# Two-layer block kernel: three quantised blocks of each batch made in earlier loops and passed through DRAM, and the weights' quantiser moved to another tile ring

## The chip, the cores and the metric

The kernel runs on one NeuronCore of a Trainium2 chip. The metric is the device time of one execution in microseconds (us). The engines are named as the profile names them: PE (TensorE, matrix products), DVE (VectorE), ACT (ScalarE), POOL (GpSimd) and SP (SyncE, which here only issues DMAs).

## The reference

The input x has 2 batches of 4096 tokens with 512 channels, in float32. Two layers follow each other; each adds two branches, which read the same layer norm, to the residual stream. Of the first layer the second branch is what the change is about:

```python
xn = _layernorm(x, axis=-1)
x = x + _L0_attn_ref(xn, ...) + _L0_ffn_ref(xn, L0_ffn_weight, L0_ffn_bias)
xn = _layernorm(x, axis=-1)
x = x + _L1_attn_ref(xn, ...) + _L1_ffn_ref(xn, ...)
# _L0_attn_ref: (ssm(silu(conv3(xn @ w1.T + b))) * silu(xn @ v1.T + b)) @ w2.T + b
# _L0_ffn_ref:  per token, blocks of 32 channels:
scales = jnp.maximum(jnp.max(jnp.abs(blocks), axis=-1) / 7.5, eps)
q = _nearest_on_grid(blocks / scales[..., None], _GRID)     # 6-bit floats
out = (xq * xs) @ (wq * ws).T + bias       # x and the weight quantised alike
# _L1_attn_ref: linear attention (16 heads, relu q and k), residual, layer norm
# _L1_ffn_ref:  sigmoid(xr @ Wr.T) * (relu(xk @ Wk.T) ** 2 @ Wv.T), xr and xk mixed with the token before
```

## The kernel before, in words

Tokens are handled in blocks of T = 512 (four tiles of 128 tokens, TJ = 4): NB = 8 blocks a batch, NK = 16 in all. The program has these stages, one after the other.

1. The first stage (the loop `for n in range(NK)`, to about 462 us) turns the normalised block (`turned`), multiplies it with w1 and v1 (`projected`, L338 and L353 take the results out of the accumulator banks on ACT), convolves the block before (`convolved`) and stores the results to DRAM. In iterations 9 to 12 it also quantises the second branch's weight, a quarter each (`quantised_weight`), and in iterations 6 to 13 the eight tiles of blocks 0 and 1 of batch 0 (`quantised`).
2. The recurrence of the state space model (to about 635 us).
3. For each batch: `mixed` computes the first layer's sum x1 block by block (`branch`, L629, is the quantised product; `x1_of` adds the product with w2, L644, and takes the bank out with L651 on POOL and L652 on DVE), normalises it and multiplies it with Wk and the keys' sums (`summed`, L675; L706 and L707 make the keys). `pairs` computes the queries and the second layer's ffn keys for two blocks at a time. `layer1` finishes the second layer, one block of 512 tokens at a time (`at_block(i)` is called at the head of each), and stores the output.

`quantised(n, j, dst, temp)` makes one tile of 128 tokens in four steps, as a generator: load the tile `xq` (L367, SP); normalise it in four pieces on ACT (L126) and find the scales of its blocks (L174 to L177 on DVE) and scale it (L178, POOL); round it (L186 to L191 on DVE, L192 on POOL); transpose it on DVE (L374) into `dst`. `quantised_weight` does the same with a tile `w_y` of the weight (L359, L362).

Where a tile is quantised: for batch 0, blocks 0 and 1 in the first stage; for batch 1, block 0 in `pairs` of batch 0 (`at_pair`). All other blocks are quantised in `mixed` itself. There a small planner sets the order: `clock` starts at -8 and `tick()` adds one, and each step of tile j of block m is due at `2 * TJ * (m - 2) + 2 * j - 2 + step`. What is due before the clock's start comes at once:

```python
clock, events = [-2 * TJ], defaultdict(list)
...
for m in range(ahead, NB):
    for j in range(TJ):
        q = quantised(b * NB + m, j, partial(xd_of, m, j), t2q)
```

`ahead` is the number of blocks that come ready made (2 for batch 0, 1 for batch 1). For these, `mixed` begins the banks with the quantised product (`branch`) before anything else.

Tiles come from rings of a fixed number of slots; a new tile waits until the slot's last user is done. Those that matter: `yv`, eight tiles of 128 x 512 (the diff calls it by that name; two are `heads`, four are `xd0`, the rest serve `xq` and the loads of `gated`); `xc`, four tiles in the first stage, used by the convolution and by `w_y`; `xe`, two tiles in the first stage, the scratch of the rounding; `t2q`, two tiles, the scratch of the rounding in the later stages and of `mixed_r` in `pairs`; `t8`, five tiles of 1 MB, for whole blocks.

A compiler orders each engine's instructions from the program's order and its own estimate of when operands are ready, so that an instruction may stand before others that the source has earlier. The trace shows it: the first tile `xq`, due in iteration 6, is loaded at 80.7 us, when the loop is in iteration 2. On each engine the order is then fixed, and an instruction that waits holds those behind it. SP issues all loads and most stores, ACT the stores of `projected` and `pairs`.

Of the kernel before, what the change touches and what calls it, by code (L numbers as in the profile page):

```python
# [10 lines left out]
F32 = mybir.dt.float32  # L11
# [32 lines left out]
def block_kernel(ctx: ExitStack, tc: tile.TileContext, a: dict, out: bass.AP):  # L44
# [28 lines left out]
    sd1 = dram.tile([NK, P, TJ, 2], F32, name="sd1")  # L73
    qd = dram.tile([NK, CC, P, T], F32, name="qd")
    kd = dram.tile([NK, CC, P, T], F32, name="kd")

    def bank(tag="mm", bufs=2):
        return ps.tile([P, D], F32, tag=tag, name=f"p_{tag}", bufs=bufs)
# [276 lines left out]
        return x1  # L355

    def quantised_weight(work, o):
        y = work.tile([P, D], F32, tag="xc", name="w_y", bufs=4)
        nc.sync.dma_start(out=y, in_=a["ffn_w"][o])  # L359
        s = mx_scaled(y)  # L360
        mx_rounded(y, s, work.tile([P, D], F32, tag="xe", name="w_c"))
        nc.vector.transpose(wd[:, :, o * P : (o + 1) * P], y)  # L362

    def quantised(n, j, dst, temp):

        xq = yv.tile([P, D], F32, tag="yv", name="xq")
        nc.sync.dma_start(out=xq, in_=a["xi"][n * TJ + j])  # L367
        yield
        laid_normalised(xq, mvi[:, :, n, j, :])
        scales = mx_scaled(xq)  # L370
        yield
        mx_rounded(xq, scales, temp())
        yield
        nc.vector.transpose(dst().rearrange("p c t -> p (c t)"), xq)  # L374
        yield

    def convolved(work, n, x1, ccs=range(CC)):
# [156 lines left out]
    def mixed(b, z0, xds, xnTs, mvs, w2, wk):  # L534
# [6 lines left out]
        def xd_of(m, j):  # L541
# [2 lines left out]
                xds[m] = [xd[:, jj] for jj in range(TJ)]  # L544
            return xds[m][j]

        clock, events = [-2 * TJ], defaultdict(list)
# [117 lines left out]
        def summed(i, j, xn, kt):  # L667
# [6 lines left out]
            for c in range(CC):  # L674
                nc.tensor.matmul(  # L675
                    pg[c], lhsT=xn[:, c * P : (c + 1) * P], rhs=kt, start=first, stop=last
                )

        x_of(0)
        x_of(1)  # L680
        for i in range(ahead):

            pos[i] = [bank(("mm", "tr")[i]) if j < 2 else acc() for j in range(TJ)]
            for j in range(TJ):
                branch(i, j, pos[i][j])
                if i == 0:
                    tick()
        x1_of(0)
        for i in range(NB):
            xn = xts[i]  # L690
            for j in range(TJ):
                rescaled(xn[j], xn[j], mvs[:, i, j, :])
            if i + 1 < NB:
                x1_of(i + 1)
            else:
                for _ in range(TJ):
                    tick()
            if i == 0:
                first_x1_turned(xn)
            xnT = xnTs[i]  # L700
            for j in range(TJ):
                tj = slice(1 + j * P, 1 + (j + 1) * P)
                pk = bank("tr")
                product(pk, lambda k: xnT[:, k, tj], lambda k: wk[:, k, :])
                kt = t2("k")
                nc.vector.tensor_tensor(kt, pk, bk, ALU.add)  # L706
                nc.scalar.activation(kt, kt, AF.Relu)  # L707
                flush()
                later.append(partial(summed, i, j, xn[j], kt))
                gate(i + 2, j)  # L710
                tick()
            if i + 2 < NB:
                x_of(i + 2)
# [112 lines left out]
    def pairs(b, xnTs, wq, wk, made, kvx, at_pair):  # L826
# [37 lines left out]
        def mixed_r(p):  # L864
            for n in range(2):
                xnT = xnTs[2 * p + n]
                for c in range(CC):
                    t = t2q()
                    nc.scalar.activation(t, xnT[:, c, 0:T], AF.Copy, scale=om_r[:, c, :])
                    nc.vector.scalar_tensor_tensor(  # L870
                        xnT[:, c, 1 : T + 1], xnT[:, c, 1 : T + 1], mu_r[:, c, :], t,
                        ALU.mult, ALU.add,
                    )
# [103 lines left out]
    with tc.tile_pool(name="tab", bufs=1) as tab:  # L977
# [3 lines left out]
        with pool("a", 2) as work, pool("pm", 1) as pm:  # L981
# [31 lines left out]
            made = []  # L1013
            powers = chunk_powers(pm, made)
            xd0 = [yv.tile([P, CC, P], F32, tag="yv", name=f"xd{j}") for j in range(TJ)]
            for n in range(NK):
                if 0 < n < NK - 1:
                    xi = laid(work, n + 1)
                if n + 3 < NK:
                    xts[n + 3] = fetched(work, n + 3)  # L1020
                before, x1 = x1, projected(work, n, xnT, x1)
                if n + 2 < NK:
                    measured(n + 2, xts.pop(n + 2))
                    spread_out(mvi[:, :, n + 2], sd[n + 2], mv0[:, n + 2])
                if n + 1 < NK:
                    xnT = turned(work, n + 1, xi)
                if 0 < n < NK - 1:
                    convolved(work, n - 1, before)
                if n in (2, 3, 8):
                    next(powers)  # L1030
                elif 4 <= n < 4 + CC:
                    chunk_tables(*made, n - 4)
                elif 9 <= n < 9 + CC:
                    quantised_weight(work, n - 9)
                if 6 <= n < 6 + 2 * TJ:

                    m, j = divmod(n - 6, TJ)
                    if m == 1 and j == 0:
                        xd_b1 = by_tile(single.tile([P, CC * (T + 1)], F32, name="wide"))
                    for _ in quantised(  # L1040
                        m, j, lambda: xd_b1[:, j] if m else xd0[j],
                        lambda: work.tile([P, D], F32, tag="xe", name="c"),
                    ):
                        pass
                if n == NK - 2:
                    b_out = load_row("w2_b")
                    ffn_b = work.tile([P, D], F32, tag="xe", name="ffn_b")
                    nc.sync.dma_start(out=ffn_b, in_=a["ffn_b"].partition_broadcast(P))
                    nc.gpsimd.tensor_tensor(b_out, b_out, ffn_b, ALU.add)
                    bk, gamma, beta = (load_row(s) for s in ("bk", "gamma", "beta"))  # L1050
                    bq, mu_r, mu_k = column("bq"), column("mu_r"), column("mu_k")
                    om_r = const.tile([P, CC, 1], F32, name="om_r")
                    om_k = const.tile([P, CC, 1], F32, name="om_k")
                    nc.vector.tensor_scalar(om_r, mu_r, -1.0, 1.0, ALU.mult, ALU.add)
                    nc.vector.tensor_scalar(om_k, mu_k, -1.0, 1.0, ALU.mult, ALU.add)
# [7 lines left out]
    z0 = t8()  # L1063
    for cc in range(CC):
        gated(0, 0, z0, cc)
    xds = {0: xd0, 1: [xd_b1[:, j] for j in range(TJ)]}

    for b in range(B):
        mvs = stay.tile([P, NB, TJ, 2], F32, tag="mvs", name="mvs")
# [5 lines left out]
        c_wts = []  # L1075
        if b + 1 < B:
            xd0 = [yv.tile([P, CC, P], F32, tag="yv", name=f"xd{j}") for j in range(TJ)]
            ahead = [quantised((b + 1) * NB, j, lambda j=j: xd0[j], t2q) for j in range(TJ)]

        def at_pair(p, half):  # L1080

            if b + 1 < B and p < TJ:
                for _ in range(2):
                    next(ahead[p])

        def at_block(i):
            if b + 1 < B and i == NB - 1:
                next_in.append(t8())
                for cc in range(CC):
                    gated(b + 1, 0, next_in[0], cc)  # L1090
# [2 lines left out]
        pairs(b, xnTs, wq, wk1, made, kvx, at_pair)  # L1093
        layer1(b, xnTs, mvs, kvx, [load_weight(s) for s in ("W_r", "W_v")], at_block)
        if b + 1 < B:
            z0, xds = next_in[0], {0: xd0}
            c_wts = [load_weight("w2_w"), load_weight("Wk")]


# [59 lines left out]
```

## Time and profile before

| | us |
|---|---|
| median of 3 runs | 2420.28 |
| lowest and highest | 2420.0, 2421.31 |
| the profiled execution | 2425.51 |
| its span, first to last instruction | 2423.7 |
| mean granted clock of PE | 0.993 |

The page of the profile has the busy time of each engine over the span; PE's matrix products and its weight loads (PEld) overlap. The stages in this execution: the first to 462 us, the recurrence to 635, `mixed` of batch 0 to 1065, `pairs` to 1262, `layer1` to 1512, and for batch 1 `mixed` to 1970, `pairs` to 2170, `layer1` to the end. A group of instructions is written as line, engine, operation, out<-in, shapes and count, then busy us, mean ns of one, and the engine's idle time just before them with what ended it. In a list of waits, "PE p_mm L629 <- DVE x L652" is read: PE's instruction of line 629, which writes the tile p_mm, could start only when DVE's of line 652 was done.

### The profile page before, as it was taken

Reading aid. Unit: us, or ns where it says so; the run is one execution under the profiler, and the core shown is the slowest. Engines: PE = TensorE matmul, PEld = TensorE weight load, DVE = VectorE, ACT = ScalarE, POOL = GpSimd, SP = SyncE. Lnnn points to the kernel's source line nnn. Section 1 sums busy time; section 2 is a strip of 40 time slices with the busy share of each in tenths; the row PEclk is TensorE's granted clock in tenths of the full one; section 3 lists DMA queues with packets and bytes.
Section 4 is the critical chain, followed back from the end, with each engine's and each line's share of the span. In section 5 each row is a group of like instructions: output and inputs, shape, how many; then the busy total and the mean of one; then the engine's idle time right before and its main releaser. Section 6 shows DMA issues by size and latency. Waiting matters only on the chain.

```text
span 2423.7 us, 21898 instructions
## 1 busy us (share of the span) xinstructions
PE 2366.3 (98%) x6400; PEld 1112.2 (46%) x6400; DVE 1545.7 (64%) x3092; ACT 1018.1 (42%) x1940; POOL 466.7 (19%) x447
## 2 busy tenths in 40 slices
PE   7999999999989999999999999799999999999999
PEld 3444443466434444444445554344444444445554
DVE  7856457565596662257658779865662265557777
ACT  5777664344342332246662223232332146662222
POOL 1000012122253331110001114333331110001111
PEclk9999999999999999999999999899999999999999
DMA  7746432477743332202264344533332202263331
GB/s 241 222 122 214 143 122 93 134 213 264 261 143 113 109 116 85 66 27 91 87 250 155 119 141 147 169 109 109 110 121 75 66 26 87 83 226 133 131 128 61
DMA packets 250521, 321.83 MB, mean 133 GB/s; under 512 B 55712, under 2 KB 117152, under 8 KB 249376
## 3 DMA queue, kind: packets, MB, share of 16 engines
q1 hardware_dynamic: 221312, 253.30, 33.0%
q10 hardware_dynamic: 29088, 67.12, 7.1%
q8 instruction: 51, 0.84, 0.1%
q14 instruction: 70, 0.57, 0.1%
HBM read 202.23 MB, written 118.12 MB: 132 GB/s over the span
## 4 chain that ended last, share of the span: by engine, by line
PE 64%; DVE 5%; issue 1%; POOL 0%; DMA 0%; ACT 0%; POOLq 0%; DVEq 0%
PE p_acc L152 16%; PE p_tr L152 9%; PE p_acc L675 8%; PE p_mm L629 7%; PE p_acc L797 7%; PE p_mm L644 7%; PE p_mm L797 6%; PE p_tr L797 2%; PE p_mm L924 1%; PE p_tr L924 1%; DVE xq L190 0%; DVE t L532 0%; DVE x L960 0%; DVE t L944 0%; POOL xq L178 0%
## 5 line engine op out<-in xcount | busy, mean ns | idle before, releaser
L152 PE MATMUL p_acc<-xnT,w_v_w 128*128 128x512 f32 x512 | 227.5, 603 | 8.1 <-ACT x L338 8.1
L675 PE MATMUL p_acc<-k,x 128*128 128x512 f32 x512 | 230.2, 593 | 3.2 <-ACT k L707 3.2
L152 PE MATMUL p_acc<-xnT,w_w_w 128*128 128x512 f32 x512 | 226.0, 600 | 5.9 <-DVE mv L122 5.0
L152 PE MATMUL p_acc<-w_W_v,t 128*128 128x512 f32 x512 | 222.3, 593 | 0.0
L629 PE MATMUL p_mm<-w_d,t 128*128 128x512 f32 x416 | 193.9, 609 | 16.3 <-DVE x L652 16.3
L152 PE MATMUL p_acc<-w_W_r,xnT 128*128 128x512 f32 x448 | 201.4, 593 | 0.0
L644 PE MATMUL p_mm<-w_w_w,t 128*128 128x512 f32 x448 | 201.1, 593 | 0.0
L152 PE MATMUL p_tr<-w_Wk,xnT 128*128 128x512 f32 x448 | 199.1, 593 | 0.0
L945 POOL TENSOR_TENSOR x<-x,row_beta 128x512 f32<-128x512 f32 x64 | 83.9, 1312 | 578.9 <-ACT xn L126 575.8
L152 PEld LDWEIGHTS p_acc<-xnT,w_v_w 128*128 128x128 f32 x512 | 98.9, 194 | 134.2 <-issue 120.3
L386 DVE SCALAR_TENSOR_TENSOR xc<-x,col_conv_w,xc 128x512 f32<-128x512 f32 x128 | 92.2, 767 | 106.4 <-POOL x L328 95.3
L152 PEld LDWEIGHTS p_acc<-xnT,w_w_w 128*128 128x128 f32 x512 | 98.5, 193 | 130.8 <-issue 119.5
L675 PEld LDWEIGHTS p_acc<-k,x 128*128 128x128 f32 x512 | 97.2, 190 | 126.5 <-issue 119.6
L673 POOL TENSOR_TENSOR ksum<-ksum,k 128x512 f32<-128x512 f32 x62 | 83.8, 1352 | 370.0 <-ACT k L707 370.0
L152 PEld LDWEIGHTS p_acc<-w_W_v,t 128*128 128x128 f32 x512 | 97.5, 190 | 122.2 <-issue 119.4
L109 ACT ACTIVATE rs_s<-rs_v 128x4 f32<-128x4 f32 x48 | 9.5, 204 | 339.6 <-DVE rs_v L107 339.4
L706 DVE TENSOR_TENSOR k<-p_tr,row_bk 128x512 f32<-128x512 f32 x64 | 43.8, 684 | 162.1 <-PE p_tr L152 162.1
L951 ACT ACTIVATE r<-p_acc 128x512 f32<-128x512 f32 x64 | 38.2, 597 | 253.3 <-PE p_acc L152 240.0
L629 PEld LDWEIGHTS p_mm<-w_d,t 128*128 128x128 f32 x416 | 80.5, 196 | 118.5 <-issue 96.6
L644 PEld LDWEIGHTS p_mm<-w_w_w,t 128*128 128x128 f32 x448 | 85.4, 191 | 107.2 <-issue 107.0
L152 PEld LDWEIGHTS p_tr<-w_Wk,xnT 128*128 128x128 f32 x448 | 85.3, 190 | 107.0 <-issue 104.3
L652 DVE TENSOR_TENSOR x<-x,p_mm 128x512 f32<-128x512 f32 x56 | 38.3, 684 | 147.9 <-PE p_mm L644 147.9
(217 smaller groups left out, 4037.8 us busy)
## 6 DMA issues: line engine op xcount, KB each, us to landing
x<-in_x SPq DMA_DIRECT2D x126, 256.0 KB, 3.5
vd<-v ACTq DMA_DIRECT2D x64, 256.0 KB, 2.7
cd<-xs SPq DMA_DIRECT2D x64, 256.0 KB, 2.7
xq<-in_xi SPq DMA_DIRECT2D x64, 256.0 KB, 4.2
xg<-cd SPq DMA_DIRECT2D x16, 1024.0 KB, 7.8
v<-vd SPq DMA_DIRECT2D x64, 256.0 KB, 4.2
xd<-x SPq DMA_DIRECT2D x64, 256.0 KB, 2.0
qd<-q ACTq DMA_DIRECT2D x64, 256.0 KB, 2.0
```

Of the source, the lines that this page charges most:

```text
L152: nc.tensor.matmul(out_ap, lhsT=lhsT(k), rhs=rhs(k), start=(k == 0), stop=(k == CC - 1))
L386: nc.vector.scalar_tensor_tensor(xc, x1[:, cc, tap : tap + T], conv_w[:, cc, tap : tap + 1], xc, ALU.mult, ALU.add,)
L629: nc.tensor.matmul(po, lhsT=xds[i][j][:, k, :], rhs=wd[:, k, :], start=(k == 0), stop=False)
L644: nc.tensor.matmul(po, lhsT=z[:, k, j * P : (j + 1) * P], rhs=w2[:, k, :], start=False, stop=(k == CC - 1),)
L652: nc.vector.tensor_tensor(xt[j], xt[j], po, ALU.add)
L673: nc.gpsimd.tensor_tensor(ksum, ksum, kt, ALU.add)
L675: nc.tensor.matmul(pg[c], lhsT=xn[:, c * P : (c + 1) * P], rhs=kt, start=first, stop=last)
L706: nc.vector.tensor_tensor(kt, pk, bk, ALU.add)
L797: nc.tensor.matmul(banks[c], lhsT=lhsT(k, c), rhs=rhs(k), start=first and k == 0, stop=k == 1, skip_group_check=True,)
L924: nc.tensor.matmul(pc[:, c, :], lhsT=qT[:, 2 * c2 + c, tj], rhs=kvx[:, 2 * c2 + c, :], start=True, stop=True,)
L945: nc.gpsimd.tensor_tensor(xt[j], xt[j], beta, ALU.add)
L951: nc.scalar.activation(r, pr, AF.Sigmoid)
```

## The change

Block 2 of batch 0 is now quantised in the first stage (iterations 13 and 14, two tiles each); blocks 1 and 2 of batch 1 in `pairs` and in `layer1` of batch 0. A tile that is made with no destination is transposed into a scratch tile and stored to the new DRAM tensor `xqd`; `xd_read` loads a whole block of it into a `t8` tile in `mixed`. Batch 1 thus begins `mixed` with the quantised products of two blocks, as batch 0 does. The weights' quantiser takes `w_y` from the ring `yv` in place of `xc`, and `mixed_r` takes its scratch from `yv` in place of `t2q`.

```diff
+    xqd = dram.tile([NK, TJ, P, D], F32, name="xqd")
...
     def quantised_weight(work, o):
-        y = work.tile([P, D], F32, tag="xc", name="w_y", bufs=4)
+        y = yv.tile([P, D], F32, tag="yv", name="w_y")
...
-        nc.vector.transpose(dst().rearrange("p c t -> p (c t)"), xq)
+        xd = dst().rearrange("p c t -> p (c t)") if dst else temp()
+        nc.vector.transpose(xd, xq)
+        if not dst:
+            nc.sync.dma_start(out=xqd[n, j], in_=xd)
...
+        def xd_read(m):
+            xd = t8((P, TJ, D))
+            nc.sync.dma_start(out=xd, in_=xqd[b * NB + m].rearrange("j p d -> p j d"))
+            xds[m] = [xd[:, j].rearrange("p (c t) -> p c t", t=P) for j in range(TJ)]
...
+        if not xds[1]:
+            xd_read(1)
         x_of(0)
         x_of(1)
-        for i in range(ahead):
+        for i in range(2):
...
         x1_of(0)
+        xd_read(2)
...
-                    t = t2q()
+                    t = yv.tile([P, T], F32, tag="yv", name="t")
...
+            def quantise(m, j, dst):
+                for _ in quantised(
+                    m, j, dst, lambda: work.tile([P, D], F32, tag="xe", name="c")
+                ):
+                    pass
...
-                    for _ in quantised(
-                        m, j, lambda: xd_b1[:, j] if m else xd0[j],
-                        lambda: work.tile([P, D], F32, tag="xe", name="c"),
-                    ):
-                        pass
+                    quantise(m, j, lambda: xd_b1[:, j] if m else xd0[j])
+                if n in (NK - 3, NK - 2):
+
+                    for j in range(2):
+                        quantise(2, 2 * (n - NK + 3) + j, None)
...
-    xds = {0: xd0, 1: [xd_b1[:, j] for j in range(TJ)]}
+    xds = {0: xd0, 1: [xd_b1[:, j] for j in range(TJ)], 2: None}
...
-            ahead = [quantised((b + 1) * NB, j, lambda j=j: xd0[j], t2q) for j in range(TJ)]
+            ahead = [
+                [quantised((b + 1) * NB + m, j, None if m else lambda j=j: xd0[j], t2q)
+                 for j in range(TJ)]
+                for m in range(3)
+            ]
 
         def at_pair(p, half):
 
-            if b + 1 < B and p < TJ:
+            if b + 1 < B:
+                for m in range(2):
+                    for _ in range(2):
+                        next(ahead[m][p])
+
+        def at_block(i):
+
+            if b + 1 < B:
                 for _ in range(2):
-                    next(ahead[p])
-
-        def at_block(i):
+                    next(ahead[2][i // 2])
...
-            z0, xds = next_in[0], {0: xd0}
+            z0, xds = next_in[0], {0: xd0, 1: None, 2: None}
```

## The prediction

> **What bounds the kernel now.** I read the page's first two parts, then what TensorE (PE) waits for, then busy time by stage, then the groups and waits of the stages that the change touches.
>
> ```profile
> span 2423.7 us, 21898 instructions
> ...
> PE 2366.3 (98%) x6400; PEld 1112.2 (46%) x6400; DVE 1545.7 (64%) x3092; ACT 1018.1 (42%) x1940; POOL 466.7 (19%) x447
> ```
>
> PE is the bound: 2366.3 of 2423.7 us. What can be won is where it waits:
>
> ```profile
> PE p_mm L629 <- DVE x L652: 16.3, 4, 6.9
> PE p_tr L146 <- DVE xn L301: 9.7, 1, 9.7
> PE p_acc L152 <- ACT x L338: 8.1, 3, 4.3
> PE p_tr L440 <- DVE h L452: 5.7, 3, 2.6
> PE p_acc L152 <- DVE mv L122: 5.0, 1, 5.0
> PE p_acc L675 <- ACT k L707: 3.2, 3, 1.5
> ```
>
> (Columns: total us, times, longest.) With four smaller ones the waits sum to 52.2 us. Three concern the change: 16.3 us at the start of `mixed` (a bank is not emptied, L652, before the next block's branch, L629, wants it), 3.2 us in its first K product, 8.1 us late in the first stage. Busy time by stage, columns window, length, PE, PEld, DVE, ACT, POOL, granted clock, DMA share, GB/s:
>
> ```profile
> 640.00:740.00 100.00, 92.35 (x220) 40.35 (x219) 88.28 (x181) 41.47 (x91) 43.38 (x39) 0.98 0.48 150
> 740.00:1065.00 325.00, 325.00 (x758) 144.06 (x757) 153.82 (x286) 94.44 (x209) 92.62 (x78) 1.00 0.30 89
> 1065.00:1262.00 197.00, 196.04 (x486) 88.84 (x485) 134.29 (x234) 128.73 (x216) 7.60 (x7) 1.00 0.32 119
> ...
> 1520.00:1580.00 60.00, 46.83 (x100) 20.20 (x99) 50.43 (x103) 16.63 (x37) 22.96 (x20) 0.89 0.51 167
> ...
> 1325.00:1356.00 31.00, 31.00 (x97) 15.73 (x96) 23.98 (x57) 8.07 (x11) 5.07 (x4) 1.00 0.39 133
> ...
> 1480.00:1512.00 32.00, 31.61 (x98) 15.80 (x97) 31.64 (x70) 7.49 (x10) 18.20 (x14) 1.00 0.35 118
> ```
>
> VectorE (DVE) is nearly full where `mixed` starts (640 to 740 for batch 0, 1512 to 1580 for batch 1), and there PE stalls and its clock dips to 0.89. In the rest of `mixed` (740 to 1065), in `pairs` (1065 to 1262) and in `layer1` (1325 to 1356 is one block) PE is gapless with DVE at 47%, 68% and 77%. In the first stage the cause is another:
>
> ```profile
> ACT xc L382 <- DVE w_d L362: 30.4, 4, 10.5
> ```
>
> ScalarE (ACT) waits four times for the weights' quantiser (L362), because `w_y` sits in the convolution's ring of four `xc` tiles. Queued behind that wait on ACT are the evacuations x L338, and PE waits for those (the 8.1).
>
> **Price of one quantised tile.** From the rows of tile xq, 640 to 745, medians: L174 0.67, L186 0.43, L190 0.69, L191 0.68, L374 0.71; with L175 0.17, L177 0.24, L189 0.41 that is DVE 4.0 to 4.2 us, taken as 4.2. POOL 2 x 1.05 = 2.1. ACT four pieces at a pitch of 0.39 = 1.6. SP one 256 KB load, landing in 3 to 4. The new way through DRAM adds a store per tile (the like xd<-x: 2.0 us) and a 1 MB read per block (the like t<-qd, t<-kd: 6.7 and 7.7): 12 stores and 3 reads, 6 MB on 322 MB, no bound.
>
> **Start of `mixed`, batch 1.** Eight tiles go (blocks 1 and 2): 8 x 4.2 = 33.6 us of DVE that was spread over about 1485 to 1586. PE stands 13.2 us there, and
>
> ```profile
> L629 PE MATMUL p_mm<-w_d,t 128*128 128x512 f32 x32 | 18.6, 733 | 13.2 <-DVE x L652 13.2
> ```
>
> the matmuls after the gaps are slow: (733 - 593) ns x 32 = 4.5. In all 17.7. Afterwards PE runs both branches first (2 x 13.7), then both blocks of L644 (2 x 13.7), 55 us without need of a fresh bank; DVE has for that time the rest of layer 1 (13 us to 1525), four gates of 1.4 and eight evacuations with statistics of 1.5, some 31 us. L652 is no longer late. Late next is what batch 0 shows with this same order: p_tr L146 waited 1.3 for its copy and K waited 3.2. I leave 4 standing: gain 13.7. The new read of block 1 must land by 1526 (the second branch). Its ring slot (t8) is freed by layer 1's block 6, before 1500, and behind it on SP's queue are the loads of x. The first branch, 13.7 us, covers its 8; without that cover it costs 8.
>
> **Start of `mixed`, batch 0.** Four tiles go: 16.8 of DVE's 88.3. Waits here: L652 3.1, k L707 3.2, and 2.2 of slow matmuls (the whole L629 group: (609 - 593) x 416 = 6.7, less 4.5), together 8.5. But twelve tiles ran between 640 and 745, blocks 2 to 4: the compiled order pulls tiles forward wherever DVE looks free, and can refill what the change frees. Bounds 0 and 8.5; I take 5. Block 2's read is wanted only after x1 of block 1, 27 us later.
>
> **First stage.** `w_y` leaves the ring: the wait of 30.4 goes, with it the 8.1 of PE and the slow matmuls behind (w_v_w 603 against 593 ns, x512: 5.1), 13.2 in all. Against it, four tiles in iterations 13 and 14: DVE 16.8, ACT 6.4, POOL 8.4. From 386 to 462 DVE is busy 46.0 of 76; it becomes 62.8, ACT 33 becomes 40. Each store waits on SP for the transpose; behind it are the load of xi(15) and the convolution's stores. ACT's scaling waits for the load, and behind it are evacuations again. No row shows four such chains here. The nearest: the last tile now, 407 to 413, held DVE 5.9 us with 2.4 of it idle for POOL, and PE had no wait after 404.5. Bounds: gain 13.2 with all hidden; loss 6 if two chains of iteration 14 (12) lie bare to half. I take 4 given back: gain 9.
>
> **Pairs and `layer1`, batch 0.** `pairs` gets four tiles: DVE 134 to 151 of 197, ACT 129 to 135. It already hides four without a wait. `mixed_r` exchanges one ring with two free slots for another (8 less 4 for xd0, less 2 in work). `layer1` gets half a tile a block: 2.1 on 24.0 of 31, or 84%. The row of 1480 to 1512 is the witness: three tiles pulled forward, DVE 31.6 of 32, and PE waited 0.4. Those three are gone afterwards. Price nothing; if the cover failed, up to 4.2 a tile, 17 for each loop. Below nothing is excluded, since PE has no wait there.
>
> [...] The rows: L190 median 0.69, longest 1.37, L191 0.68 and 1.64 where POOL was 43% busy, mean 0.80, so some 0.2 us a tile, 1 in all. [...]
>
> [...]
>
> [...]
>
> **Sum.** 13.7 + 5 + 9 = 27.7 us. The profiled execution took 2425.5 (span 2423.7 and 1.8 around it), so 2397.8 for its like; the median of the runs is 5.2 lower, so 2420.3 - 27.7 = 2392.6, about 2393.
>
> **Rivals.** (1) The first stage gives nothing: its four chains cost what the ring gave (9 to 15 instead of 4). 2420.3 - 18.7 = 2402, with the loss of 6, 2408. For it: SP and ACT wait in order. Against: DVE idles 30 of the 76 us. (2) The change only moves the crowd: blocks 3 and 4 are pulled into the room freed at the start of `mixed`, L652 stays late, and of the first stage's 9 layer1 takes 5: 2416. For: twelve tiles in 640 to 745. Against: in batch 1 the order of PE alone brings 27 us of cover. (3) Slower: slots of the ring of single tiles. Of eight, two (heads) and four (xd0) are held, so two pass `w_y` and `xq`, two a block from iteration 9, five in the last two. Blocks last 27.5 us, so a tile may stay 27.5; beyond, SP stands at the load with xi and the stores behind it, and the block grows to the stay. `w_y` stays 12.4 now (358.5 to 370.9). Two chains in a row, the next load (4.2) and the convolution's transposes in front (4) make 33: 6 blocks x 5.5 = 33, and 2420.3 - 18.7 + 33 = 2435. For it: the loads of xq come in pairs now (293.9, 294.4, then 310.2, 310.7). Against: the two chains interleave.
>
> **Chances.** Forecast 0.63 (2380 to 2402), rival 1 0.20, rival 2 0.07, rival 3 0.10. 0.2% is 4.8 us, about what a measurement can tell from none. Faster 0.83, same 0.07, slower 0.10. All targeted losses gone is 17.7 + 8.5 + 13.2 = 39.4, or 2381. The range 2380 to 2414 holds forecast and rival 1 and leaves out 2 and 3.
>
> **What would show it.** Right: p_mm L629 <- DVE x L652 below 3 us, xc L382 <- DVE w_d L362 gone, PE in 1520 to 1580 at full clock, no new wait above 1 us in `pairs` and `layer1`. Wrong: waits on PE between 385 and 470 above 4 us (rival 1), L652 still above 10 (rival 2), loads L359 or L367 standing on SP and PE waiting for xnT after 300 us (rival 3), a PE wait for the block read into xd.

## The result, and the profile after

The changed kernel takes 2403.22 us in the median of 6 runs (2399.11 to 2405.67), against 2420.8 for the kernel before in 6 runs (2419.4 to 2426.88): a ratio of 0.9922, 95% interval 0.9907 to 0.9936. The gain is 17.6 us between the medians and 19.9 us between the spans of the two profiled executions; the forecast was 27.7. The time lies in the stated range, 2380 to 2414. It lies just outside the 2380 to 2402 that the prediction kept for its own forecast, and where its rival 1 (the first stage gives nothing, 2402) put it. What the forecast overstated is found stage by stage below.

The first two parts of the page of after:

```profile
span 2403.8 us, 21932 instructions
...
PE 2361.7 (98%) x6400; PEld 1107.3 (46%) x6400; DVE 1542.3 (64%) x3092; ACT 1016.9 (42%) x1940; POOL 464.3 (19%) x447
```

Every engine has as much work as before. PE's waits, from the list for the whole span (total us, times, longest). Lines have moved: L152 is now L153, L338 and L353 are L339 and L354, L629 and L652 are L638 and L661:

```profile
PE p_tr L147 <- DVE xn L302: 9.5, 1, 9.5
PE p_acc L153 <- ACT v L354: 6.4, 3, 3.2
PE p_tr L444 <- DVE h L456: 5.7, 3, 2.6
PE p_acc L153 <- DVE mv L123: 5.0, 1, 5.0
PE p_acc L153 <- ACT x L339: 2.8, 3, 1.7
PE p_acc L809 <- ACT t L816: 2.6, 2, 1.8
PE p_tr L153 <- DVE kvx L751: 2.0, 4, 0.7
PE p_mm L638 <- DVE x L661: 1.0, 1, 1.0
PE p_acc L684 <- ACT k L719: 0.9, 1, 0.9
```

Three readings. The bank that `mixed` waited for (16.3 before) waits 1.0, and the keys 0.9 instead of 3.2. In the first stage the 8.1 behind `x` has fallen to 2.8, but 6.4 behind `v`, which was not in the list before, has come: 9.2 in all. And `pairs` (L809) has a wait of 2.6 that it did not have. Busy time by stage (window, length, PE, PEld, DVE, ACT, POOL, granted clock, DMA share, GB/s), three of the stages that the prediction showed (`pairs` starts some 3 us sooner now):

```profile
640.00:740.00 100.00, 97.72 (x237) 43.02 (x236) 77.68 (x155) 35.45 (x77) 38.64 (x34) 1.00 0.51 168
...
1062.00:1262.00 200.00, 196.39 (x490) 88.85 (x489) 147.08 (x268) 130.92 (x230) 16.32 (x15) 1.00 0.34 126
...
1520.00:1580.00 60.00, 60.00 (x153) 27.49 (x152) 37.59 (x77) 18.12 (x36) 12.69 (x12) 1.00 0.35 112
```

In 1520 to 1580 PE is busy 60.00 of 60 at full clock, where it had 46.83 at 0.89. DVE has 37.59 of work there instead of 50.43. At the start of `mixed` of batch 0 PE has gone from 92.35 to 97.72 of 100. ACT's waits in the first stage (180 to 462 us):

```profile
...
ACT xi L127 <- DMA xi<-in_xi: 29.1, 6, 10.1
ACT xc L394 <- DVE xc L390: 14.5, 10, 4.4
...
ACT xq L127 <- DMA xq<-in_xi: 7.3, 1, 7.3
```

The wait of 30.4 us for `w_d` is gone. PE's waits in that stage are not.

The stages side by side. Each ends with a PE instruction of its own, so its length can be read from the trace. The first number is counted from a gap of 5.0 us that PE has at the start of iteration 1: in all the runs here that gap begins between 41.7 and 44.4 us (43.6 before, 43.7 after), and what lies ahead of it is no part of the change. The recurrence is counted to PE's last product of it, at 619.1 us before and 621.3 after; the 635 given further up was rough, and the time from 619 on is counted to `mixed`.

| stage, us | before | after | difference | forecast |
|---|---|---|---|---|
| first stage and recurrence | 575.6 | 577.6 | +2.0 | -9 |
| `mixed`, batch 0 | 445.5 | 438.1 | -7.4 | -5 |
| `pairs`, batch 0 | 198.6 | 201.9 | +3.3 | 0 |
| `layer1`, batch 0 | 249.7 | 249.1 | -0.6 | 0 |
| `mixed`, batch 1 | 458.9 | 441.5 | -17.4 | -13.7 |
| `pairs` and `layer1`, batch 1 | 451.9 | 451.9 | 0 | 0 |

`mixed` won more than forecast in both batches (24.8 for 18.7). The first stage won nothing, and `pairs` lost 3.3.

Where the first stage waits is the surprise. The prediction looked for trouble in iterations 13 and 14, after 385 us. PE's waits lie between 264 and 362 us, and in 386 to 462 PE is busy 76.00 of 76 (DVE 35.58, where 62.8 had been expected). The rows of `xqd` and `w_y` say why (duration ns min/median/max, first and last start in us):

```profile
L378 SPq DMA_DIRECT2D xqd<-c x4: 319/323/327, 327.6 to 350.5; - x4
```

```profile
L360 SPq DMA_DIRECT2D w_y<-in_ffn_w x4: 351/386/504, 225.4 to 273.4; - x4
```

```profile
L359 SPq DMA_DIRECT2D w_y<-in_ffn_w x4: 426/680/1019, 293.3 to 389.8; - x4
```

The first two are of after, the third of before. The four tiles written in the source for iterations 13 and 14 are stored from 328 to 351 us, in iterations 10 and 11. The first of the weight's four quarters is loaded 68 us sooner than before, the last 116. Once no ring of the convolution holds them back, the compiled order pulls them forward, into the stretch where blocks 0 and 1 are being quantised.

One gap followed back. The timeline of after from 296 to 306 us (start, duration, engine, line, operation, out<-in, count, and the idle time before with what ended it):

```profile
297.93 0.43 DVE L187 TENSOR_SCALAR c<-xq 128x512 int32<-128x512 int32 x1 [1.22 <-POOL xq L179]
...
300.42 1.05 POOL L193 TENSOR_TENSOR xq<-xq,mx_s 128x512 f32<-128x512 f32 x1 [2.52 <-DVE xq L192]
...
301.41 0.19 POOL L329 COPY x<-x 128x4 f32<-128x4 f32 x1
...
301.50 0.71 DVE L376 STREAM_TRANSPOSE wide<-xq 128x512 f32<-128x512 f32 x1 [1.23 <-POOL xq L193]
302.13 2.70 DVE L390 SCALAR_TENSOR_TENSOR xc<-x,col_conv_w,xc 128x512 f32<-128x512 f32 x4
302.88 1.29 ACT L394 ACTIVATE xc<-xc 128x512 f32<-128x512 f32 x2 [3.13 <-DVE xc L390]
...
304.98 0.67 ACT L354 ACTIVATE v<-p_acc,col_v_b 128x512 f32<-128x512 f32 x1
...
305.70 1.22 PE L153 MATMUL p_acc<-xnT,w_w_w 128*128 128x512 f32 x1 [3.19 <-ACT v L354]
```

Read it from the bottom. PE stood 3.19 us for the evacuation L354 on ACT. L354 stood in ACT's queue behind the convolution's L394, which itself had waited 3.13 for DVE's taps L390. The taps stood in DVE's queue behind the transpose L376 of a quantised tile, which waited 1.23 for POOL's multiplication L193. The taps also need the halo copy L329, and that stands behind L193 in POOL's queue. The list of waits names only "ACT v"; the reason lies three queues back. Whether it is the cause is what the last experiments test.

### The profile page after: what moved, and what is told of

Read it like the earlier page. It is cut to its first block, busy times and chain, and to the rows that moved or that the text cites. A ratio compares the mean times of both kernels' runs of the same rounds, so it can differ in the third digit from the quotient of the medians.

```text
span 2403.8 us, 21932 instructions
## 1 busy us (share of the span) xinstructions
PE 2361.7 (98%) x6400; PEld 1107.3 (46%) x6400; DVE 1542.3 (64%) x3092; ACT 1016.9 (42%) x1940; POOL 464.3 (19%) x447
## 4 chain that ended last, share of the span: by engine, by line
PE 67%; DVE 4%; DMA 1%; issue 1%; ACT 1%; POOL 1%; SPq 0%; POOLq 0%; ACTq 0%; DVEq 0%
PE p_acc L153 18%; PE p_tr L153 8%; PE p_acc L684 8%; PE p_mm L653 7%; PE p_mm L638 7%; PE p_mm L809 6%; PE p_acc L809 6%; PE p_tr L809 2%; PE p_mm L936 1%; PE p_tr L936 1%; PE p_acc L638 1%; PE p_acc L653 1%; PE p_tr L653 1%; PE p_tr L638 1%; DMA xq<-in_xi 0%
## 5 line engine op out<-in xcount | busy, mean ns | idle before, releaser
L153 PE MATMUL p_acc<-xnT,w_w_w 128*128 128x512 f32 x512 | 231.6, 612 | 12.1 <-ACT v L354 6.4
L153 PE MATMUL p_acc<-xnT,w_v_w 128*128 128x512 f32 x512 | 223.4, 593 | 2.8 <-ACT x L339 2.8
L153 PE MATMUL p_acc<-w_W_v,t 128*128 128x512 f32 x512 | 222.3, 592 | 0.0
L153 PE MATMUL p_acc<-w_W_r,xnT 128*128 128x512 f32 x448 | 201.4, 592 | 0.0
L153 PE MATMUL p_tr<-w_Wk,xnT 128*128 128x512 f32 x448 | 199.2, 592 | 0.1
L653 PE MATMUL p_mm<-w_w_w,t 128*128 128x512 f32 x416 | 186.7, 592 | 0.0
L638 PE MATMUL p_mm<-w_d,t 128*128 128x512 f32 x384 | 173.6, 593 | 1.2 <-DVE x L661 1.0
L153 PEld LDWEIGHTS p_acc<-xnT,w_w_w 128*128 128x128 f32 x512 | 99.6, 196 | 141.9 <-issue 120.5
L153 PEld LDWEIGHTS p_acc<-xnT,w_v_w 128*128 128x128 f32 x512 | 96.8, 190 | 127.0 <-issue 114.3
L153 PEld LDWEIGHTS p_acc<-w_W_v,t 128*128 128x128 f32 x512 | 97.3, 190 | 122.5 <-issue 119.1
L390 DVE SCALAR_TENSOR_TENSOR xc<-x,col_conv_w,xc 128x512 f32<-128x512 f32 x128 | 91.4, 765 | 89.8 <-POOL x L329 88.0
L718 DVE TENSOR_TENSOR k<-p_tr,row_bk 128x512 f32<-128x512 f32 x64 | 43.8, 684 | 162.1 <-PE p_tr L153 162.1
L179 POOL TENSOR_TENSOR xq<-xq,mx_rs 128x512 f32<-128x512 f32 x64 | 76.3, 1192 | 303.6 <-DVE mx_rs L178 219.3
L153 PEld LDWEIGHTS p_tr<-w_Wk,xnT 128*128 128x128 f32 x448 | 85.0, 190 | 107.6 <-issue 104.0
L719 ACT ACTIVATE k<-k 128x512 f32<-128x512 f32 x64 | 40.1, 627 | 203.1 <-DVE k L718 203.1
L653 PEld LDWEIGHTS p_mm<-w_w_w,t 128*128 128x128 f32 x416 | 79.0, 190 | 99.5 <-issue 99.5
```

The costliest lines, as they stand in the source:

```text
L153: nc.tensor.matmul(out_ap, lhsT=lhsT(k), rhs=rhs(k), start=(k == 0), stop=(k == CC - 1))
L179: nc.gpsimd.tensor_tensor(by_block(y), by_block(y), rs.unsqueeze(2).to_broadcast([P, NQ, QB]), ALU.mult)
L390: nc.vector.scalar_tensor_tensor(xc, x1[:, cc, tap : tap + T], conv_w[:, cc, tap : tap + 1], xc, ALU.mult, ALU.add,)
L638: nc.tensor.matmul(po, lhsT=xds[i][j][:, k, :], rhs=wd[:, k, :], start=(k == 0), stop=False)
L653: nc.tensor.matmul(po, lhsT=z[:, k, j * P : (j + 1) * P], rhs=w2[:, k, :], start=False, stop=(k == CC - 1),)
```

## The experiments

Each of the twelve kernels computes the whole reference. Times are medians, ratios are to the kernel before on the same chip with the 95% interval, stages are as in the table above.

| kernel | us | ratio | first stage + recurrence | `mixed` 0 | `pairs` 0 | `layer1` 0 | `mixed` 1 |
|---|---|---|---|---|---|---|---|
| before | 2420.8 | | 575.6 | 445.5 | 198.6 | 249.7 | 458.9 |
| after | 2403.2 | 0.9922 | 577.6 | 438.1 | 201.9 | 249.1 | 441.5 |
| ring_only | 2420.2 | 0.9984 [0.9977, 0.9991] | 571.4 | 445.7 | 198.6 | 251.0 | 459.6 |
| ring_back | 2404.9 | 0.9923 [0.9909, 0.9938] | 577.9 | 438.3 | 201.7 | 249.1 | 441.2 |
| b0_late | 2405.5 | 0.9922 [0.9907, 0.9937] | 570.3 | 445.4 | 202.2 | 249.1 | 441.5 |
| mixr_back | 2404.9 | 0.9926 [0.9909, 0.9942] | 574.0 | 437.8 | 198.6 | 254.6 | 441.4 |
| one_slot | 2405.9 | 0.9931 [0.9915, 0.9948] | 577.9 | 438.6 | 201.8 | 249.1 | 441.4 |
| rec | 2402.4 | 0.9924 [0.9904, 0.9944] | 573.8 | 438.1 | 201.8 | 249.1 | 441.5 |
| mixr_t2 | 2411.1 | 0.9957 [0.9940, 0.9973] | 574.0 | 446.9 | 200.4 | 248.7 | 441.5 |
| combo | 2414.1 | 0.9968 [0.9956, 0.9979] | 577.5 | 447.1 | 200.5 | 248.7 | 441.3 |
| vec | 2392.7 | 0.9872 [0.9858, 0.9887] | 563.9 | 439.4 | 201.8 | 249.1 | 441.5 |
| b1_two | 2402.4 | 0.9914 [0.9897, 0.9930] | 573.6 | 438.6 | 200.8 | 248.7 | 441.5 |
| vec_before | 2411.7 | 0.9954 [0.9938, 0.9971] | 563.9 | 445.4 | 198.6 | 250.5 | 457.2 |
| best | 2388.7 | 0.9865 [0.9850, 0.9880] | 566.3 | 440.0 | 198.6 | 248.7 | 441.9 |

A caution for the fourth column. Up to 800 us, every engine of mixr_back, mixr_t2 and b1_two runs the same instructions in the same order as in after, and yet they show 574.0, 574.0 and 573.6 for its 577.6. One profile's first stage is thus good to some 4 us, and "the first stage won nothing" means +2 by after's own profile, about -2 by the three others. The spread is not in the waits: PE waits 9.2 us in this stage in after and 10.2 in mixr_back, but the product with `w_w_w` behind the waits takes 612 ns in the mean in after and 600 in mixr_back (x512). The later stages of like kernels repeat within 1 to 2 us.

**ring_only.** The kernel before with the weight's ring alone.

```diff
-        y = work.tile([P, D], F32, tag="xc", name="w_y", bufs=4)
+        y = yv.tile([P, D], F32, tag="yv", name="w_y")
```

> The kernel before with one line of the change: w_y from the ring of single tiles. In the changed kernel the first stage and the recurrence took 621.3 us, where before they took 619.1: ACT's wait for w_d (30.4 us) is gone, and yet nothing was won, since PE waits 9.3 us between 264 and 361 us, where it did not wait before. Theory 1 (the ring does both): freed of the convolution's ring, the weights' tiles are pulled forward to 225 to 300 us with the tiles of x, and crowd ACT and DVE there; then this kernel too gains nothing in the first stage, PE waits on ACT's v and x between 225 and 330, and the time is within 3 us of before, 2418 to 2424. Theory 2 (the four added tiles make the crowd): without them the ring's gain of about 13 us is seen, the recurrence ends near 607, and the time is 2407 to 2411.

The stage gained 4 us of the 13.2 that the prediction saw freed (571.4 for 575.6), and the whole kernel 0.9984: 3.8 us between the medians of 20 and 23 runs, so the gain is small but clear. PE's waits in the first stage fell from 8.1 to 6.3 and changed their names:

```profile
PE p_acc L152 <- ACT v L353: 4.3, 2, 3.1
...
PE p_acc L152 <- ACT x L338: 2.0, 2, 1.6
```

They now lie at 262 to 304 us, where after's begin, and this kernel has no block 2 in the first stage. So the new place of the waits comes with the ring.

**ring_back.** The changed kernel with the weight back in the convolution's ring (the same edit, reversed).

> The changed kernel with w_y back in the convolution's ring. Theory 1: ACT waits for w_d again, some 30 us in all, the crowd at 264 to 361 thins out, and the stage takes what it took, the end of the recurrence within 3 us of 621; time 2400 to 2407. Theory 2: the four tiles come on top of the old waits, 6 to 13 us more, 2409 to 2416.

Time and first stage are those of after (577.9 for 577.6). PE's longer waits move again, to 368 to 422 us, and ACT has its wait for `w_d` back, 28.8 us. With twelve tiles of x in the stage, the ring is worth nothing that shows beyond the spread of 4 us.

**b0_late.** Block 2 of batch 0 quantised in `mixed` again; all else as in after.

```diff
-        xd_read(2)
+        if 2 in xds and not xds[2]:
+            xd_read(2)
...
-                if n in (NK - 3, NK - 2):
-
-                    for j in range(2):
-                        quantise(2, 2 * (n - NK + 3) + j, None)
...
-    xds = {0: xd0, 1: [xd_b1[:, j] for j in range(TJ)], 2: None}
+    xds = {0: xd0, 1: [xd_b1[:, j] for j in range(TJ)]}
```

> The changed kernel, but block 2 of batch 0 is quantised in mixed again, as before. Mixed of batch 0 took 438.1 us with the change and 445.5 before. If the four tiles taken out are what gave these 7.4 us, they come back here. Theory 1: the first stage stays at 621 to 623, so the time is 2408 to 2413. Theory 2: the first stage gains 9 to 13 without the four tiles, and the time is 2396 to 2402.

`mixed` gives back its 7.3 us; the first stage is shorter by 7.3 than in after, by 3.3 to 3.7 than in the three other runs with after's first stage. The time, 2405.5, lies between the ranges of both theories, and the ratio is that of after, 0.9922. Four tiles cost the first stage about what they give `mixed`.

**mixr_back.** The scratch of `mixed_r` from its old ring.

```diff
-                    t = yv.tile([P, T], F32, tag="yv", name="t")
+                    t = t2q()
```

> The changed kernel with the scratch of mixed_r back in its ring of two. Pairs of batch 0 took 201.9 us with the change and 198.6 before, with two PE waits on ACT's t (1.8 and 0.8). If the shared ring of single tiles makes them (its slots are held by tiles xq for a whole pair), they go and the time is 2399 to 2402. If the four tiles of block 1 make them by their work on DVE and ACT, nothing changes or it gets worse, because the scratch of the rounding uses the same two slots: 2402 to 2408.

`pairs` is back at 198.6: its loss was this edit alone. In after, ACT's L881, which writes the scratch, waits for a quantised tile to leave the ring, and the evacuations L816 stand behind it in ACT's queue. ACT's wait list of after in `pairs`:

```profile
ACT t L881 <- DVE mx_c L376: 4.6, 3, 3.4
```

But `layer1` loses 5.5 in its place, with one new wait on PE:

```profile
PE p_tr L936 <- DVE den L945: 3.9, 1, 3.9
```

So the total stays, and only half of the expectation came true. The wait ends at 1295.9 us. The last three tiles of block 2 are stored from 1282.6 to 1303.7, and DVE's `den` L945 stands behind their steps; in after the last is stored at 1289.9. The run best, below, shows that the 5.5 need these tiles.

**one_slot.** My next theory was that the pulled-forward tiles crowd DVE. All sixteen quantised tiles of the first stage (weight and input) share a ring of one slot, so that only one is under way.

```diff
-        y = yv.tile([P, D], F32, tag="yv", name="w_y")
+        y = work.tile([P, D], F32, tag="mxq", name="w_y", bufs=1)
...
-        xq = yv.tile([P, D], F32, tag="yv", name="xq")
+        xq = ring() if ring else yv.tile([P, D], F32, tag="yv", name="xq")
...
+                    lambda: work.tile([P, D], F32, tag="mxq", name="xq", bufs=1),
```

> The changed kernel, with all sixteen quantised tiles of the first stage (four of the weight, twelve of x) in a ring of one slot, so that only one is on its way at a time. With the change DVE was busy 46.0 us of the stretch 250 to 306, before 25.4, and PE waited 6.3 there. If it is the pulling forward in bunches that costs (theory 1), DVE's share is spread out, PE waits less than 4 us between 100 and 460, the recurrence ends 5 to 9 us earlier, at 612 to 616, and the time is 2394 to 2399. If each tile costs PE something wherever it lies (theory 2), or if one slot holds up SP with the loads of xi behind it, the recurrence ends at 621 or later and the time is 2403 to 2415.

It spread the work and did nothing for the time. The window 250 to 306 us, and PE's waits in 100 to 470, of one_slot:

```profile
250.00:306.00 56.00, 50.41 (x116) 21.43 (x115) 33.37 (x58) 32.01 (x69) 9.58 (x11) 1.00 0.30 101
```

```profile
PE p_acc L153 <- ACT v L354: 7.5, 4, 2.7
PE p_acc L153 <- ACT x L339: 4.5, 4, 1.8
```

DVE has 33.37 us of work there (46.03 in after), PE is busy 50.41 us, hardly more than in after (49.69), and waits 12.0 in all. So thinning out the crowd is not enough. It isn't a clean test, though: with one slot DVE also waits longer for POOL's multiplications, 28.4 us in 180 to 462 instead of 18.4. The clean test of the crowd is vec, below.

**rec.** Block 2 of batch 0 in the recurrence instead, four tiles spread over eight of its steps.

```diff
+        tiles = [
+            quantised(2, j, None, lambda: work.tile([P, D], F32, tag="xe", name="c", bufs=1))
+            for j in range(TJ)
+        ]
...
+            if step[0] and step[1] % 2 == 0 and step[0] <= 2:
+                k = 2 * (step[0] - 1) + step[1] // 2
+                for _ in range(2):
+                    next(tiles[k])
...
-                if n in (NK - 3, NK - 2):
-
-                    for j in range(2):
-                        quantise(2, 2 * (n - NK + 3) + j, None)
```

> The changed kernel, with block 2 of batch 0 quantised during the recurrence, one tile each at four places of its second and third quarter (scratch of one slot there), and not in the first stage. Leaving them in mixed (b0_late) ended the recurrence 7.0 us earlier and made mixed of batch 0 7.3 longer. If the first stage is the wrong place for them only because of its crowd, the recurrence here ends near 614, mixed keeps its 438 us, and the time is 2395 to 2398. If four tiles of 4.2 us of DVE cost PE as much in the recurrence, where DVE is busy 57% and PE waits for the states h, the recurrence grows from 138 by 3 to 7 us and the time is 2399 to 2404.

The recurrence grew from 138.1 to 142.8, with waits that after has none of:

```profile
PE p_acc L484 <- DVE h L456: 4.9, 4, 1.8
```

In sum it is the same as after. The four tiles have their price here too, some 5 us.

**mixr_t2.** The scratch of `mixed_r` from a third ring.

```diff
-                    t = yv.tile([P, T], F32, tag="yv", name="t")
+                    t = t2("t")
```

> The changed kernel, with the scratch of mixed_r from the ring t2 of four tiles (queries and keys on their way out) in place of the ring of single tiles. With that ring pairs of batch 0 took 201.9 us, with the ring of two 198.6, but then layer1 took 5.5 more, with one PE wait of 3.9 at its start. If the shortage of slots makes the waits of pairs, they go here (198.6). If the wait at the start of layer1 comes from the tiles of block 1 that the ring of two holds back past the end of pairs, it does not come here (249): 2398 to 2401. If the stores of queries and keys hold t2, pairs waits again, 2403 to 2408.

That missed. `pairs` fell only to 200.4, and `mixed` of batch 0 grew by 8.8, 6.0 of them in one wait at 953 us, long before `pairs`:

```profile
PE p_acc L684 <- ACT k L719: 6.9, 2, 6.0
```

The trace tells more than the name of the wait. With `mixed_r` out of the ring of single tiles, its slots let the compiled order pull all twelve tiles of batch 1 forward into `mixed` of batch 0, from 911 to 1006 us. In after two of them are loaded there, and the rest follow from `pairs` on. From 925 to 965 us DVE is busy 32.82 us in mixr_t2 and 15.79 in after, PE 34.00 and 40.00. L718 on DVE, for which k L719 waits, stands behind the tiles' steps. No run puts the tiles back with this ring, so this is a reading of the trace and not a test.

**combo.** one_slot, rec and mixr_t2 together.

> The three edits together: one slot for the twelve quantised tiles that stay in the first stage, block 2 of batch 0 in the recurrence, the scratch of mixed_r from t2. If each saves what theory 1 says and they add up (first stage 5 to 9, pairs 3.3, the four tiles nothing anywhere), the recurrence ends at 608 to 614, pairs take 198.6, and the time is 2388 to 2394. If the gains exclude each other, 2395 to 2402.

It missed as well: 2414.1, with the losses of rec (recurrence 144.0) and mixr_t2 (`mixed` 447.1) added. Its first stage and recurrence take 577.5 and rec's 573.8, so one slot for the twelve tiles that stay wins nothing either.

**vec.** A new theory, from the timeline above: not how much DVE has to do, but that each chain goes DVE, POOL, DVE, POOL, DVE, and DVE or the halo copies wait in order for POOL's multiplications. So both multiplications go to DVE, in the first stage only. This gives DVE more to do.

```diff
+    mul = [nc.vector]
...
-        nc.gpsimd.tensor_tensor(
+        mul[0].tensor_tensor(
...
+        mul[0] = nc.gpsimd
         with pool("s", 2) as work:
```

> The changed kernel, with the two multiplications of each quantised tile of the first stage on DVE in place of POOL (the later stages keep POOL). In one gap of PE that was followed back (302.5 us, 3.2 long) v L354 on ACT stood behind the convolution's L394, which waited 3.1 for DVE's L390, and that stood behind a tile xq, for which DVE twice waited 1.2 for POOL. Theory A (the waits for POOL inside the chains hold up the convolution on DVE): without them the chains close up, PE waits less than 4 us between 100 and 460, the recurrence ends at 611 to 616, and the time is 2394 to 2398. Theory B (it is DVE's work in front of the convolution, whatever it waits for): 16 tiles x 1.4 us = 22 us more of it on DVE, the recurrence ends at 623 to 630, and the time is 2405 to 2412.

2392.7 us, 10.6 below after and a little below what theory A forecast; the recurrence ends at 605.8, sooner than it forecast. The first stage is 13.7 shorter than in after, about 10 shorter than in its three repetitions. The window and PE's waits as for one_slot:

```profile
250.00:306.00 56.00, 54.78 (x128) 23.84 (x127) 51.64 (x106) 41.81 (x87) 0.87 (x3) 1.00 0.46 156
```

```profile
PE p_acc L153 <- ACT v L356: 1.2, 1, 1.2
PE p_acc L153 <- ACT x L341: 1.1, 1, 1.1
```

DVE is at 51.64 of 56, the fullest of all the runs in that window, and PE waits 2.3 in the stage where it waited 9.2. Here the theory of the crowd falls. The rest of the 13.7 is in the products with `w_w_w`, which take 224.8 us in all instead of 231.6. In after, 32 of them take 16.99 us behind the gap of 3.19 us, and 32 behind a gap of 1.22 take 14.00. In after, DVE's waits for POOL's multiplications between 250 and 362 us were:

```profile
DVE c L376 <- POOL xq L193: 5.6, 4, 1.9
DVE c L187 <- POOL xq L179: 5.1, 5, 1.2
DVE wide L376 <- POOL xq L193: 2.1, 3, 1.2
...
DVE w_d L363 <- POOL w_y L193: 1.2, 2, 0.9
DVE w_c L187 <- POOL w_y L179: 1.2, 1, 1.2
```

With one more of 0.9 that is 16.1 us; in vec there are none. (DVE still waits for POOL's halo copies in vec, 7.2 us in this window.) The same multiplication takes 1.05 us on POOL in after and 0.68 on DVE in vec, but POOL was not short of time: from 250 to 306 us of after it was busy 16.49 of 56. What cost, by these runs, was that DVE's queue stood still while POOL multiplied, the 16.1 us above.

**vec_before.** The same edit in the kernel before.

> The kernel before, with nothing of the change, but the two multiplications of the first stage's quantised tiles on DVE. It tells whether the waits for POOL also made the old losses of the first stage. If the wait of ACT for w_d (30.4 us) is long mainly because w_y's chain waits for POOL, its 12 tiles lose less: the recurrence ends at 606 to 612 and the time is 2408 to 2415. If the shared ring alone makes the loss, it ends at 617 to 623 and the time is 2418 to 2424.

The first stage falls to 563.9, by 11.7, with `w_y` still in the convolution's ring, and the time is in the first of the two ranges. ACT still waits 19.2 us for `w_d` there, and PE 1.6 instead of 8.1:

```profile
ACT xc L384 <- DVE w_d L364: 19.2, 4, 7.5
```

```profile
PE p_acc L152 <- ACT x L340: 1.1, 1, 1.1
PE p_acc L152 <- ACT v L355: 0.5, 1, 0.5
```

So the wait that the prediction read as the fault of the ring was long enough to hurt because the chains waited for POOL.

**b1_two.** Batch 1 begins with two blocks ready (0 and 1); its block 2 is quantised in `mixed` again.

```diff
...
-                for m in range(3)
+                for m in range(2)
...
-            if b + 1 < B:
-                for _ in range(2):
-                    next(ahead[2][i // 2])
...
-            z0, xds = next_in[0], {0: xd0, 1: None, 2: None}
+            z0, xds = next_in[0], {0: xd0, 1: None}
```

> The changed kernel, but block 2 of batch 1 is quantised in mixed again; block 1 still comes through DRAM, so that PE begins with two branches. It splits the 17.4 us that mixed of batch 1 won. If the order of PE with two branches first is what takes the long waits away (the prediction's reason), the start then looks like batch 0's before (8.5 to 10 us of waits there): mixed of batch 1 takes 449 to 451, and the time is 2410 to 2414. If most of the gain came from block 2's tiles, the long waits of 6 us come back and it takes 455 to 459, 2416 to 2422. If block 2 was a passenger, it stays at 442 to 444.

`mixed` of batch 1 keeps its 441.5. Its first stretch:

```profile
1520.00:1580.00 60.00, 60.00 (x153) 27.45 (x152) 45.47 (x93) 19.84 (x41) 16.84 (x16) 1.00 0.38 123
```

DVE has 7.88 us more to do in it than in after, and PE still has no gap. Block 2 through DRAM is a passenger. The order of PE and the four tiles of block 1, which must be ready for it, go together here, and no run parts them. But the load of DVE is hardly what they change. The stretch around the start, first of before, then of b1_two:

```profile
1500.00:1600.00 100.00, 86.83 (x206) 38.69 (x205) 79.01 (x168) 27.61 (x56) 30.76 (x28) 0.93 0.44 142
```

```profile
1500.00:1600.00 100.00, 100.00 (x246) 45.20 (x245) 79.44 (x150) 36.65 (x82) 38.62 (x33) 1.00 0.46 153
```

DVE is as busy as before, 79 of 100 us, and PE has lost its 13.2 us of gaps. It is the same if each is counted for 60 us from its own start of `mixed`: DVE 53.18 before, 52.95 in b1_two. With two branches ready PE can go on while DVE catches up.

**best.** What the runs spoke for: vec, b1_two, and `mixed_r` back in its old ring.

> The changed kernel with DVE's multiplications in the first stage, block 2 of batch 1 back in mixed (it was a passenger), and the scratch of mixed_r in its old ring of two (pairs 198.6 in place of 201.8). layer1 grew by 5.5 with that ring when it held tiles of block 2; without those it should stay at 249. If so, the time is 2387 to 2391. If the wait at the start of layer1 belongs to block 1's tiles, layer1 takes 254 and the time is 2391 to 2396.

2388.7 us (2387.5 to 2393.1), 0.9865 [0.9850, 0.9880]: faster than both kernels. `pairs` is at 198.6 and `layer1` at 248.7, so the 5.5 of mixr_back do not appear when block 2's tiles are not there. The step beyond vec (0.9872) is smaller than the intervals and isn't established.

## Why the prediction came out as it did, point by point

- **Start of `mixed`, batch 1: right, 17.4 for 13.7.** The mechanism is the one given: PE runs two branches first, and L661 is no longer late. The 4 us kept back for what would be late next were not needed. Of the "eight tiles" that go, four do nothing: b1_two leaves block 2's in and wins the same, with DVE as busy as before. Block 1's four count as what makes the second branch ready.
- **The read of block 1: right.** It is issued at 1481.7 and has landed at 1487.6, long before the second branch at about 1524, and PE doesn't wait for it.
- **Start of `mixed`, batch 0: right, 7.4 for 5,** near the upper bound of 8.5. L661 and K wait 1.0 and 0.9. Rival 2, the crowd that only moves, fell.
- **First stage: wrong, +2 (or -2) for -9.** Two terms failed. "With it the 8.1 of PE and the slow matmuls behind, 13.2 in all" was mis-sized: ring_only shows some 4, since other waits took the place of the old ones. The four tiles, taken at 4, cost 3 to 7 (b0_late), less than the 9 to 15 that rival 1 gave them. So the ring's gain and the tiles' cost cancel, as rival 1 has it, but both are smaller than it said, and not where it looked (after 385 us). The step behind both was the reading of the cause: the wait for `w_d` was taken as a matter of the ring's slots. vec and vec_before show that PE waits in this stage because quantised chains go through POOL, whichever ring they have: with the multiplications on DVE it waits 2.3 us for 9.2, and 1.6 for 8.1. The nearest row in the prediction, a tile that "held DVE 5.9 us with 2.4 of it idle for POOL", had this in it; it was used as a price for four tiles and not asked of the twelve others.
- **Pairs: wrong, +3.3 for 0.** The term that failed is "`mixed_r` exchanges one ring with two free slots for another". The slots were not free when ACT wanted them (4.6 us of waits for L376), and banks stand behind it (2.6 on PE). The four quantised tiles themselves cost `pairs` nothing (mixr_back: 198.6).
- **`layer1`: right in the number, by luck in the reason.** No "half a tile a block" came. The compiled order put block 2's four tiles at the seam after `pairs`, stored from 1256.4 to 1289.9, and the row of 1480 to 1512 has none of the added tiles in it (DVE 29.66 of 32, PE 32.00). At the seam they cost nothing in after and 5.5 in mixr_back.
- **Rival 3, SP standing at a full ring, fell.** In PE's list of after no wait for `xnT` is longer than 0.7 us.
- **The clock.** The rows put 13.2 of waiting and 4.5 of slow matmuls at the start of `mixed`, 17.7; 17.4 came back, and the granted clock in 1520 to 1580 went from 0.89 to 1.00. Before, the gaps there were 6.90 and 6.27 us, and the eight matmuls of L629 behind each took 5.15 and 6.23 us; eight with no gap in front took 3.60. At the start of `mixed` of batch 0, again before, a gap of 2.45 us also had a slow run behind it, 5.40 for eight.
- **POOL beside DVE.** The "0.2 us a tile", what L190 and L191 took on average beyond their medians, counts two instructions of eight. In the same list L186 has a mean of 0.66 for its median of 0.43, and L175 0.37 for 0.17, so it is some 0.6 us a tile. In `pairs` of before, where POOL was busy 7.60 of 197 us, the longest L190 of four took 0.69 and the longest L186 0.43; that POOL makes the difference is an estimate from these rows, and no run tests it alone. In `layer1` the 0.6 is still nothing for PE, which waits 0.2 us in all there (1262 to 1512 us of after).

In sum: 24.8 from `mixed` for 18.7, 3.3 lost in `pairs`, 2.0 in the first stage, 0.6 won in `layer1`: 20.1, against 19.9 between the spans. That the time fell in the range is in part luck: the 6 us won beyond the forecast in `mixed` made up for half of the 11 that the first stage missed.

**What stays open.** vec takes away two things at once: DVE's waits for POOL inside the chains, and the place of the halo copies behind POOL's multiplications. At 301.4 us both end together, and no run separates them. Over 180 to 462 us DVE's waits for the halo copies hardly change (61 to 76 us in after and its repetitions, 70.9 in vec), which speaks for the chains. The compiled order of DVE, ACT and SP also changes with the edit; that two kernels with different rings gain alike (vec and vec_before) speaks against chance there. Why the order in mixr_back makes `layer1` late is not settled beyond the part of block 2's tiles, and the account of mixr_t2 is read from its trace alone.

## What to carry to other kernels

When a wait ends with an evacuation, follow the queues back past the engine that the list names: here PE waited for ACT, ACT for DVE, and DVE for POOL, and 10 to 14 us lay in a hop between two engines that were both partly idle (DVE busy 46.03 and POOL 16.49 of 56 us). The price of these chains, which change engine four times, was not their busy time but what stood in order behind each hop; with the hop moved onto the engine that waited for it the kernel was 10.6 us shorter, though that engine became fuller (DVE 51.64 of 56 us). And of a change with several parts, undo each alone: here one block made ready for PE's new order carried 17.4 us, the two other blocks that were moved gave nothing in sum, and a scratch tile's ring cost 3.3.

## What the runs showed that was not expected

The place where an instruction had been written said little about when it ran: tiles written for iterations 13 and 14 were stored in iterations 10 and 11, and in another ring the weight's four quarters started 65 to 116 us sooner. The slots of a ring acted as a brake on this. Taking a scratch that is used only in `pairs` out of the ring of single tiles let twelve tiles run in `mixed` before it, which grew by 8.8 us.
